# GpSimd multiplies one of eight state pairs with B in the scan of a four-layer image kernel

## The chip, the cores and the metric

The kernel runs on one core of one Trainium2 chip. The metric is the device time of one execution in microseconds. A core has five engines with queues of their own: TensorE (PE in the profile; PEld are its weight loads), VectorE (DVE), ScalarE (ACT), GpSimd (POOL) and SyncE (SP, which here issues the DMAs). Each engine works through its own queue in the order in which the program was written; semaphores order the work between engines.

## The reference

The input is 32 images of 128 channels and 56 x 56 pixels in fp32. Four layers follow one another, each as `x = x + layer(groupnorm(x))`: a dynamic convolution, a spline activation, a linear attention with a convolution, and a Mamba layer. The change lies in the fourth. Its core, for L = 3136 pixels taken as time, 256 inner channels d and 16 states n, is

```
delta = softplus(dt @ dt_proj_w.T + dt_proj_b)         # (L, 256)
dA    = exp(delta[..., None] * A)                      # (L, 256, 16)
dBu   = delta[..., None] * B_ssm[:, :, None, :] * xc[..., None]
h_t   = dA_t * h_{t-1} + dBu_t                         # the scan
y_t   = sum over n of h_t[d, n] * C_t[n]
```

The later `y + xc * D`, the gate `silu(z)` and the output projection follow on y.

## The kernel before

**Tiling.** An image is cut into 7 chunks of 448 pixels (CH, 8 rows of 56). Within a chunk the 256 channels x 16 states are worked off in 16 steps (STEPS): 8 pairs of states (NPAIR), and for each pair two blocks of 128 channels (DI). One step holds a tile h of 128 partitions x 2 x 448: partition halves of 64 are the two states of the pair, the middle index the two halves of the block's channels. 32 images x 7 chunks x 16 steps are 3584 steps.

**One step** (class Scan, lines 1041 to 1136). With `p, db = divmod(n, 2)`:

- `b_rows` (line 1069): once for each pair, a matmul with the selection matrix spreads the two B rows of the pair over the partitions, into the PSUM tile pb. Its pool ps_bc has one buffer (line 381).
- `c_rows` (line 1060): the same for C, into an mm tile (pool ps_mm, three buffers), which ScalarE copies to an SBUF tile cb (three buffers).
- `decay` (line 1076): ScalarE computes exp(delta * A) twice, 128x448 each, into two PSUM tiles da. Pool ps_da has two buffers, so a step takes both.
- `state` (line 1084): VectorE makes the product h = du * B over 128x896 (pb broadcast over the middle index; du is delta * xc), and then two scans over 448 in place, each with its da tile and the last value of the chunk before. h has three buffers.
- `products` (line 1100): ScalarE keeps the last column of h; GpSimd multiplies h with cb into hc (two buffers).
- `add` (line 1108): TensorE sums hc over the states into y, and at the end of the chunk VectorE applies the gate and TensorE the output projection.

Before the scan, `ssm_inputs` (line 1002) prepares a chunk: matmuls, silu, delta and du (GpSimd adds and multiplies 128x896 each) and, by DMA, the rearranged copies of delta and du that the steps read. `layer_norm` (line 964) prepares xn for the chunk after.

**Order of the work.** The loop over images (line 1284) takes six images a pass, and `images` (line 1196) writes the whole pass as a list of works: for each step the scan's own calls (lines 1254 to 1261), pieces of the next chunk's inputs, pieces of the next image's spline and attention layers, and pieces of the first layer of the image after that. Each work has a step and a lead (`plan.at(g, FIRST)`; FIRST is 8 steps, SECOND 4). The class Plan prices each work by engine and size (line 163), works out due times backward from the steps (line 232: a work is due its own cost ahead of whatever needs it), and then goes through a list schedule (`attempt`, line 245) with one queue for each engine and the buffers of each pool. Of the works that could start first on an engine the one with the earliest due time goes first; no work may be more than 12 steps ahead of the oldest one left. The result is a fixed order for each engine, which is issued at line 338; that is why nearly every row of the profile has line 338, and why rows are told apart by their tiles. Times at run time do not change the order.

Of the kernel before, what the change touches and what calls it, by code (L numbers as in the profile page):

```python
# [12 lines left out]
F32 = mybir.dt.float32  # L13
# [5 lines left out]
P = 128  # L19
# [3 lines left out]
CH = ROWS * W  # L23
# [31 lines left out]
DI = 2  # L55
# [4 lines left out]
B_ROW, C_ROW = 0, 64  # L60
# [6 lines left out]
NB = DI * P // Q  # L67
NPAIR = NST // 2
STEPS = NPAIR * DI
AHEAD = 2  # L70
LAG = 3
FIRST, SECOND = 8, 4
# [290 lines left out]
def tile_conv_stack(ctx: ExitStack, tc: tile.TileContext, out: bass.AP, x: bass.AP, w: dict):  # L363
    nc = tc.nc
# [4 lines left out]
    def pool(name, bufs, **kw):  # L369
        return Rotation(plan, ctx.enter_context(tc.tile_pool(name=name, bufs=bufs, **kw)), name, bufs)  # L370
# [5 lines left out]
    wide = pool("wide", 1)  # L376
    ssm = pool("ssm", 2)
    cbp = pool("cbp", 3)
    dramp = ctx.enter_context(tc.tile_pool(name="dramp", bufs=1, space=bass.MemoryType.DRAM))
    ps_mm = pool("ps_mm", 3, space=bass.MemoryType.PSUM)  # L380
    ps_bc = pool("ps_bc", 1, space=bass.MemoryType.PSUM)
# [179 lines left out]
    du = const.tile([P, DI, CH], F32, name="du")  # L561
# [18 lines left out]
    nc = plan  # L580

    def psum(cols=CH, rows=P):
        t = ps_mm.tile([P, 512], F32, tag="mm", name="mm")
        return t[:rows, :cols]


    class Stats:


        def __init__(self, xt, st=None):  # L590
            self.xt, self.done = xt, 0
            self.st = small.tile([P, NCH, 6], F32, tag="st", name="st") if st is None else st
# [399 lines left out]
    def gate(xn):  # L992

        for db in range(DI):
            ps = psum()
            nc.tensor.matmul(
                ps, wzT[:, db * P : (db + 1) * P], xn[:, DCONV - 1 :], start=True, stop=True
            )
            silu(sz[:, db, :], ps)
            yield 0.8  # L1000
# [40 lines left out]
    class Scan:  # L1041
# [3 lines left out]
        def __init__(self, xt, dst, last, k):  # L1045
            self.xt, self.dst, self.last, self.j, self.k = xt, dst, last, k % NCH, k
            self.dbl, self.xc = dbls[k % 2], xcs[k % 2]
            self.cbs, self.pbs, self.das, self.hcs, self.pys = {}, {}, {}, {}, {}

        def half(self, n):  # L1050

# [17 lines left out]
        def b_rows(self, n):  # L1069

            p, db = divmod(n, DI)
            if db == 0:
                self.pbs[p] = ps_bc.tile([P, 512], F32, tag="bc", name="pb")[:, :CH]
                self.both(self.pbs[p], B_ROW, p)

        def decay(self, n):
# [3 lines left out]
            for i in range(2):  # L1080
                b = 2 * db + i
                nc.scalar.activation(self.das[n][i], delta[:, i, :], AF.Exp, scale=amat[:, b, p : p + 1])

        def state(self, n):
            _, du = self.half(n)
            da = self.das.pop(n)
            h = ssm.tile([P, 2, CH], F32, tag="h", name="h", bufs=3)
            nc.vector.tensor_mul(h[:], du[:], self.pbs[n // DI].unsqueeze(1).to_broadcast([P, 2, CH]))
            for i in range(2):
                nc.vector.tensor_tensor_scan(  # L1090
                    h[:, i, :],
                    da[i],
                    h[:, i, :],
                    0.0 if self.j == 0 else self.last[:, n, i : i + 1],
                    ALU.mult,
                    ALU.add,
                )
            self.h = h

        def products(self, n):  # L1100
            h = self.h
            if self.j < NCH - 1:
                nc.scalar.copy(self.last[:, n, :], h[:, :, CH - 1])
            hc = ssm.tile([P, 2, CH], F32, tag="hc", name="hc", bufs=2)
            nc.gpsimd.tensor_mul(hc[:], h[:], self.cbs[n // DI][:].unsqueeze(1).to_broadcast([P, 2, CH]))
            self.hcs[n] = hc

        def add(self, n):
# [15 lines left out]
            if p == NPAIR - 1:  # L1124
                nc.vector.tensor_mul(sz[:, db, :], sz[:, db, :], self.pys[db])
            if n == STEPS - 1:
                cols = slice(self.j * CH, (self.j + 1) * CH)
# [5 lines left out]
        def store(self, n):  # L1133
            if n == STEPS - 1:
                cols = slice(self.j * CH, (self.j + 1) * CH)
                nc.sync.dma_start(self.dst[:, cols], self.xt[:, cols])


    def first_layer(src, b):

        xt = xts[b % 3]
        for j in range(NCH):
            nc.sync.dma_start(xt[:, j * CH : (j + 1) * CH], src[:, j * CH : (j + 1) * CH])
        yield from dynamic_conv(xt, sts[b % 2])

    def until_scan(b):

        xt = xts[b % 3]
        st = yield from spline(xt, sts[b % 2])
        st = yield from linear_attention(xt, st)  # L1150
        norm = carried[b % 2]
        norm_weights(st, *norm)
        yield 5.0
        layer_norm(xt, xns[b * NCH % 3], 0, norm)
        yield 5.0

    def first_inputs(b):
        return ssm_inputs(xts[b % 3], b * NCH, carried[b % 2])
# [37 lines left out]
    def images(first, count, ahead):  # L1196

        def image(v, b):  # L1200
            return v[:, ds(first + b, 1), :].squeeze(1)

        scans = {}

        def new_last():
            return small.tile([P, STEPS, 2], F32, tag="last", name="last")

        def at(g, what):

            if 0 <= g < count * NCH * STEPS:  # L1210
                getattr(scans[g // STEPS], what)(g % STEPS)

        plan.start(FIRST)

        for b in range(count):
            xt = xts[b % 3]
            steps = (NCH - 1) * STEPS + READY
            more = b + 1 < count or ahead
            rest = Pieces(until_scan(b + 1) if more else None, totals[1], REST)
            layer0 = Pieces(first_layer(image(xv, b + 2), b + 2) if b + 2 < count or ahead else None, totals[0], steps)  # L1220
            for j in range(NCH):
                k = b * NCH + j
                if k == 0:
                    last = new_last()
                    scans[0] = Scan(xt, image(ov, 0), last, 0)
                    for n in range(AHEAD):
                        at(n, "c_rows")
                    for n in range(2):
                        at(n, "b_rows")
                    at(0, "decay")  # L1230
                following = None
                if j + 1 < NCH:
                    following = ssm_inputs(xt, k + 1, carried[b % 2])
                elif more:
                    following = first_inputs(b + 1)
                following = Pieces(following, PREP, READY)
                gates = Pieces(gate(xns[k % 3]), 1.6, DI)
                for n in range(STEPS):
                    g = k * STEPS + n
                    plan.at(g)  # L1240
                    if n == 0 and j == NCH - 1:
                        rest.finish()
                    if n == READY:

                        following.finish()
                        gates.finish()
                        if j == NCH - 1:
                            layer0.finish()
                        if k + 1 < count * NCH:
                            nb, nj = divmod(k + 1, NCH)  # L1250
                            if nj == 0:
                                last = new_last()
                            scans[k + 1] = Scan(xts[nb % 3], image(ov, nb), last, k + 1)
                    plan.at(g, FIRST)
                    at(g + 2, "b_rows")
                    at(g, "state")
                    at(g + 1, "decay")
                    at(g, "products")
                    at(g + AHEAD, "c_rows")
                    at(g - LAG + 1, "add")  # L1260
                    at(g - LAG, "store")
                    plan.at(g, SECOND)
                    following.step(n)
                    if n >= READY - DI:
                        gates.step(n - READY + DI)
                    plan.at(g)
                    rest.step(j * STEPS + n)
                    if j * STEPS + n > LAG:
                        layer0.step(j * STEPS + n)
        end = count * NCH * STEPS  # L1270
        for g in range(end - LAG + 1, end):
            at(g, "add")
        at(end - 1, "store")
        plan.issue()
# [9 lines left out]
    with tc.For_i(0, B - 2, unroll) as i:  # L1284
        images(i, unroll, True)
    images(B - 2, 2, False)


# [100 lines left out]
```

## Time and profile before

| | |
|---|---|
| runs | 16321.42, 16330.96, 16344.79 us; median 16330.96 us |
| profiled execution | 16316.11 us, span from first to last instruction 16314.3 us |
| mean granted TensorE clock | 0.893 |
| steps | 3584, so 4.55 us of span each; a chunk takes some 72.8 us |
| matmul y<-hc,sums | 14336, 3997.9 us busy |
| decays da<-delta,alog on ScalarE | 7168, mean 633 ns, 4481.8 us busy |
| matmul pb<-dbl,sel | 1792, mean 512 ns |
| delta<-delta,du and du<-delta,xc on GpSimd | 224 each, mean 2093 and 2089 ns |
| DMA | 1589.93 MB, mean 97 GB/s |

How to read the profile: a group line gives line, engine, operation, the tiles out<-in, the shapes and the count; after the first bar the busy time in all and the mean of one in ns; after the second the engine's idle time just before such instructions and what ended most of it. A line of waits gives who waited for whom, the total in us, how often, and the longest. "hc<-h,cb" is the product with C, "h<-du,pb" the product with B, "h<-da,last,h" a scan.

### The profile page before, as it was taken

To read this page: it belongs to the slowest core of one execution; us is meant where nothing else is said; L and a number is where in the kernel's file an instruction comes from. 1 tells how busy PE (TensorE), PEld (TensorE's weight loads), DVE (VectorE), ACT (ScalarE), POOL (GpSimd) and SP (SyncE) were. 2 spreads that over 40 slices of the span, in tenths; PEclk is the share of its full clock that TensorE was granted. 3 is DMA by queue.
4 is the path that set the end of the run, shared out by engine and by line. 5 is a ranking of instruction groups with operands and counts; after the bars stand their busy time and mean duration, and the time that the engine had idled before them with its cause. 6 is when DMAs were issued, how large, how long until landed. Compare 5 with 4: busy or idle time off the path is not lost. (4 is left out here: it accounts for less than half of the span.)

```text
span 16314.3 us, 212520 instructions
## 1 busy us (share of the span) xinstructions
PE 14202.3 (87%) x66400; PEld 4559.9 (28%) x66400; DVE 14306.2 (88%) x17314; ACT 11713.4 (72%) x21127; POOL 10785.0 (66%) x6406
## 2 busy tenths in 40 slices
PE   6888898888898888988888888888888898888887
PEld 2222222222222222222222222222222222222222
DVE  2898988989889898899988888888898898888889
ACT  3777777777677776777776777767777677776675
POOL 2676666666666666667666666666676666766666
PEclk7888998889998898998989988899988899888888
DMA  6344444344443444434444434444344444344421
GB/s 143 93 101 98 98 112 96 89 99 101 106 104 88 100 97 101 109 94 94 101 99 107 102 86 98 99 105 107 91 98 97 100 108 106 85 97 99 101 56 34
DMA packets 986159, 1589.93 MB, mean 97 GB/s; under 512 B 175622, under 2 KB 611209, under 8 KB 984331
## 3 DMA queue, kind: packets, MB, share of 16 engines
q1 hardware_dynamic: 985002, 1576.06, 41.0%
q8 instruction: 538, 8.81, 0.2%
q14 instruction: 619, 5.06, 0.1%
HBM read 785.62 MB, written 173.18 MB: 59 GB/s over the span
## 5 line engine op out<-in xcount | busy, mean ns | idle before, releaser
L338 POOL TENSOR_TENSOR hc<-h,cb 128x896 f32<-128x896 f32 x3584 | 7476.1, 2092 | 4173.5 <-DVE h L338 2178.7
L338 DVE TENSOR_TENSOR_SCAN h<-da,last,h 128x448 f32<-128x448 f32 x6144 | 6772.7, 1135 | 498.2 <-ACT da L338 451.3
L338 ACT ACTIVATE da<-delta,alog 128x448 f32<-128x448 f32 x7168 | 4481.8, 633 | 2635.3 <-DVE h L338 2369.4
L338 PE MATMUL y<-hc,sums 128*64 128x448 f32 x14336 | 3997.9, 638 | 625.6 <-POOL hc L338 617.8
L338 DVE TENSOR_TENSOR h<-du,pb 128x896 f32<-128x896 f32 x3584 | 3788.6, 1072 | 247.5 <-POOL hc L338 118.2
L338 PE MATMUL mm<-stack,dsT 96*32 96x448 f32 (+1 forms) x16128 | 1890.8, 575 | 59.4 <-DMA stack<-padded 16.8
L338 ACT ACTIVATE hats<-stack,bia,scl 128x448 f32<-128x448 f32 x2688 | 1887.6, 754 | 33.9 <-DVE bia L338 31.7
L338 PE MATMUL mm<-xn,winT 128*128 128x448 f32 x3584 | 1703.8, 590 | 39.8 <-ACT cb L338 13.5
L338 PEld LDWEIGHTS y<-hc,sums 128*64 128x64 f32 x14336 | 807.6, 147 | 2412.9 <-POOL hc L338 1436.9
L338 PE MATMUL mm<-hats,wspl 128*32 128x448 f32 x12544 | 1386.1, 563 | 33.3 <-ACT hats L338 30.4
L338 PE MATMUL pb<-dbl,sel 64*128 64x448 f32 x1792 | 918.3, 512 | 421.2 <-DVE h L338 364.3
L338 ACT ACTIVATE hats<-hats,one 128x1344 f32<-128x1344 f32 x896 | 1261.5, 1408 | 0.1
L338 ACT COPY cb<-mm 128x448 f32<-128x448 f32 x1792 | 940.3, 527 | 379.4 <-POOL hc L338 184.0
L338 PE MATMUL mm<-dbl,sel 64*128 64x448 f32 x1792 | 892.3, 502 | 363.5 <-DVE sz L338 63.7
L338 ACT ACTIVATE t<-mm 128x448 f32<-128x448 f32 x1568 | 829.2, 534 | 484.6 <-PE mm L338 480.3
L338 POOL TENSOR_TENSOR xt<-xt,g 128x448 f32<-128x448 f32 x672 | 767.5, 1142 | 524.1 <-DVE g L338 491.1
L338 DVE TENSOR_TENSOR_SCAN h<-da,h 128x448 f32<-128x448 f32 x1024 | 1054.1, 1070 | 28.3 <-ACT da L338 26.3
L338 PEld LDWEIGHTS mm<-xn,winT 128*128 128x128 f32 x3584 | 631.8, 197 | 986.0 <-issue 805.1
L338 DVE SCALAR_TENSOR_TENSOR g<-t,mm 128x448 f32<-128x448 f32 x672 | 407.7, 607 | 443.7 <-ACT t L338 392.8
L338 PEld LDWEIGHTS mm<-stack,dsT 96*32 96x32 f32 (+1 forms) x16128 | 445.2, 112 | 1156.3 <-issue 899.9
L338 PEld LDWEIGHTS mm<-dbl,sel 64*128 64x128 f32 x1792 | 351.2, 198 | 1453.5 <-issue 420.0
L338 PEld LDWEIGHTS pb<-dbl,sel 64*128 64x128 f32 x1792 | 358.6, 200 | 1419.1 <-issue 791.8
(187 smaller groups left out, 16166.2 us busy)
## 6 DMA issues: line engine op xcount, KB each, us to landing
stack<-padded SPq DMA_DIRECT2D x2688, 264.0 KB
stack<-xt SPq DMA_DIRECT2D x3584, 56.0 KB
delta<-delta SPq DMA_DIRECT2D x1792, 112.0 KB
du<-du SPq DMA_DIRECT2D x1792, 112.0 KB
padded<-yc SPq DMA_DIRECT2D x224, 264.0 KB
padded<-yc SPq DMA_DIRECT2D x256, 231.0 KB
xt<-x_dram SPq DMA_DIRECT2D x224, 224.0 KB
out_dram<-xt SPq DMA_DIRECT2D x224, 224.0 KB
```

The costliest lines, as they stand in the source:

```text
L338: call()
```

## The change

A constant names the pairs that are treated in another way: pair 4 alone, which is steps 8 and 9 of each chunk. For it, the B rows go into an mm tile in place of pb, and ScalarE copies them to an SBUF tile bb (a new pool of one buffer). The product with B becomes a call of its own, `inputs`, taken out of `state`: for pair 4 it runs on GpSimd and reads bb, for the other pairs it runs on VectorE and reads pb as before. For all pairs the call now stands one step earlier in the list, between the scans of step g and the decays of step g + 1. The tile h is kept by step in a dictionary in place of one variable.

```diff
+ASIDE = (4,)
...
+    bbp = pool("bbp", len(ASIDE))
...
         def b_rows(self, n):
             p, db = divmod(n, DI)
-            if db == 0:
+            if db == 0 and p in ASIDE:
+                ps = psum()
+                self.both(ps, B_ROW, p)
+                self.bbs[p] = bbp.tile([P, CH], F32, tag="bb", name="bb")
+                nc.scalar.copy(self.bbs[p][:], ps)
+            elif db == 0:
                 self.pbs[p] = ps_bc.tile([P, 512], F32, tag="bc", name="pb")[:, :CH]
                 self.both(self.pbs[p], B_ROW, p)
...
+        def inputs(self, n):
+
+            _, du = self.half(n)
+            h = self.hs[n] = ssm.tile([P, 2, CH], F32, tag="h", name="h", bufs=3)
+            if n // DI in ASIDE:
+                nc.gpsimd.tensor_mul(h[:], du[:], self.bbs[n // DI][:].unsqueeze(1).to_broadcast([P, 2, CH]))
+            else:
+                nc.vector.tensor_mul(h[:], du[:], self.pbs[n // DI].unsqueeze(1).to_broadcast([P, 2, CH]))
+
         def state(self, n):
-            _, du = self.half(n)
             da = self.das.pop(n)
-            h = ssm.tile([P, 2, CH], F32, tag="h", name="h", bufs=3)
-            nc.vector.tensor_mul(h[:], du[:], self.pbs[n // DI].unsqueeze(1).to_broadcast([P, 2, CH]))
+            h = self.hs[n]
...
-            self.h = h
 
         def products(self, n):
-            h = self.h
+            h = self.hs.pop(n)
...
                     for n in range(2):
                         at(n, "b_rows")
+                    at(0, "inputs")
                     at(0, "decay")
...
                     at(g + 2, "b_rows")
                     at(g, "state")
+                    at(g + 1, "inputs")
                     at(g + 1, "decay")
                     at(g, "products")
```

More of the change, by code (lines that the diff above doesn't have):

```diff
@@ L1047, in __init__ @@
             self.dbl, self.xc = dbls[k % 2], xcs[k % 2]
-            self.cbs, self.pbs, self.das, self.hcs, self.pys = {}, {}, {}, {}, {}
+            self.cbs, self.bbs, self.pbs, self.das, self.hs, self.hcs, self.pys = {}, {}, {}, {}, {}, {}, {}
         def half(self, n):
```

## Prediction

> **What bounds the kernel now.** I read the page from the top: busy shares, then the chain of work that ended last, then the costliest groups.
>
> ```profile
> PE 14202.3 (87%) x66400; PEld 4559.9 (28%) x66400; DVE 14306.2 (88%) x17314; ACT 11713.4 (72%) x21127; POOL 10785.0 (66%) x6406
> ...
> DVE 9%; PE 6%; ACT 4%; issue 2%; POOL 2%; DMA 0%; SPq 0%; POOLq 0%; DVEq 0%; ACTq 0%
> ...
> L338 POOL TENSOR_TENSOR hc<-h,cb 128x896 f32<-128x896 f32 x3584 | 7476.1, 2092 | 4173.5 <-DVE h L338 2178.7
> L338 DVE TENSOR_TENSOR_SCAN h<-da,last,h 128x448 f32<-128x448 f32 x6144 | 6772.7, 1135 | 498.2 <-ACT da L338 451.3
> L338 DVE TENSOR_TENSOR h<-du,pb 128x896 f32<-128x896 f32 x3584 | 3788.6, 1072 | 247.5 <-POOL hc L338 118.2
> L338 ACT COPY cb<-mm 128x448 f32<-128x448 f32 x1792 | 940.3, 527 | 379.4 <-POOL hc L338 184.0
> ```
>
> VectorE and TensorE are both near 88% and GpSimd has a third of its time free. The chain goes back only over the last pass of the image loop and the two images after it, so its shares add up to some 24% of the span; of what it covers, VectorE holds 9 of 24 parts, TensorE 6, ScalarE 4, GpSimd 2. No single engine is the bound. Next come the waits of VectorE and TensorE:
>
> ```profile
> PE y L338 <- POOL hc L338: 617.8, 697, 6.3
> PE pb L338 <- DVE h L338: 364.3, 360, 15.8
> ...
> DVE h L338 <- ACT da L338: 478.9, 503, 3.0
> ...
> DVE h L338 <- POOL hc L338: 118.2, 93, 3.0
> ...
> DVE h L338 <- PE pb L338: 88.7, 115, 1.9
> ```
>
> The scans wait for the decays 503 times; the products with B wait rarely, for a free h buffer (GpSimd) or for pb (TensorE). Last, the table by stretches of one typical chunk (image 20, second chunk), cut at the starts of the products of steps 0, 6, 8, 10 and the next chunk's 0; each pair is busy us and instructions, for PE, PEld, DVE, ACT and POOL:
>
> ```profile
> 10494.22:10514.72 20.50, 19.89 (x106) 6.46 (x105) 20.50 (x29) 16.35 (x31) 14.23 (x10) 1.00 0.23 57
> 10514.72:10525.04 10.32, 6.24 (x18) 1.90 (x16) 10.32 (x19) 10.32 (x20) 6.86 (x4) 0.82 0.00 1
> 10525.04:10535.35 10.31, 9.65 (x23) 3.43 (x24) 10.19 (x14) 8.74 (x16) 6.39 (x4) 0.68 0.28 68
> 10535.35:10562.00 26.65, 20.41 (x94) 5.53 (x92) 21.68 (x25) 24.47 (x43) 21.02 (x14) 0.88 0.40 99
> ```
>
> Pair 4 is the third row (steps 8 and 9): VectorE is full there and GpSimd is idle for 3.9 of 10.3 us. I ordered all rows of the trace by step: over all chunks of the loop, steps 7 to 11 last 22.4 us, of which VectorE is idle 2.0 and GpSimd 9.4; in steps 12 to 14 GpSimd is idle only 1.2 of 14.8 us, because the next chunk's delta, du and xn fall there. So the chosen pair lies in a stretch where VectorE is short and GpSimd is not.
>
> **What the Trainium skill says.** "GPSIMD Engine Reference", section "Performance versus the Vector engine": a two-input elementwise instruction takes about 1.96 times as long on GpSimd. The trace agrees: 2092 ns against 1072 ns for the same 128x896 shape, 1.95. "PSUM — Partial Sum Buffer", section "PSUM: the matmul accumulator": GpSimd can't touch PSUM; hence the copy to SBUF. "Advanced Engine Details and Errata", section "Miscellaneous Facts": GpSimd shares an SBUF interface with VectorE and conflicts with VectorE instructions that have two SBUF inputs. Here the products and scans each have one operand in PSUM, and hc stays between 2061 and 2151 ns; but the small aggT<-dwT,attr,aggT on VectorE takes 0.33 us alone and 1.22 us beside an hc, so the conflict is visible on small rows. "Perfetto Trace Analysis", section "Per-instruction lifecycle": ScalarE, VectorE and GpSimd are strict FIFOs, so a late product holds back every hc behind it.
>
> **The change part by part**, against the profiled run (16316.1 us, span 16314.3; the median of the runs is 14.9 us higher).
>
> 1. VectorE loses one pair in eight: 3584 / 8 = 448 products. Start to start, a product followed at once by another instruction takes 0.998 us (median over the trace), so 447 us of VectorE work go. That all of it shows is the upper end. The nearer figure comes from the chain: in the last pass of the loop (2948 us) the chain spends 388 us in steps 8 and 9, 137 of them in h on VectorE. A product is 1.00 of 1.00 + 2 x 1.06 us of a step's h work, 0.32, so 44 us, 1.49% of the pass; times 16314 that is 243 us. With the order of work fixed the gain can't be more than that. The order isn't fixed (the planner writes it anew), and of the remaining 204 us of free VectorE time I let a quarter, 50 us, come to use. Taken: -293 us; ends -447 and 0.
>
> 2. GpSimd gains 448 x 2.092 = 937 us (busy 66% to 72%). Most lies in its idle time. Its share on the path: hc holds 3.4% of the chain in that pass and is busy 46% of the span, a ratio of 0.074, so 69 us. The conflicts with VectorE: its small rows with two SBUF inputs (vv 78, aggT 69, dm 36, ab 34, att 29 us: 246) grow with GpSimd's busy time, 937/10785 or 9%; half of the 21 us, 10. Taken: +79; ends 0 and the case of lateness below.
>
> 3. ScalarE gains 224 copies (32 images x 7 chunks), priced by the cb copy of the same shape: 224 x 0.527 = 118 us (72% to 72.5%). ScalarE holds some 15% of the chain and is busy 72%, ratio 0.21: 25 us. Behind the copy in ScalarE's queue stand decays, and behind those the scans. Taken +25; ends 0 and 118.
>
> 4. Between a step's scans and the next stood a product of 1 us, under which ScalarE made the next decays (633 ns each, and only as a scan frees one of the two PSUM buffers). In two steps of 16 this cover goes. Now 503 of 3584 steps wait, 0.95 us each; if in the 448 steps the share rises from 14% to about 30%, this is 448 x 0.16 x 0.95 = 68 us, of which other VectorE work fills half: +34. Ends 0 and 200 (half of them wait 0.95 us).
>
> 5. Buffers. The matmul for pair 4 goes from the single bc buffer to one of three mm buffers. Credit: an eighth of the pb waits, 11 us of VectorE and 45 of TensorE; debit: an mm buffer is held about 1 us once a chunk. I take 0; ends -30 and +30.
>
> 6. The products of all pairs are now issued a step earlier, ahead of that step's decays: their due time falls by some 2 us of plan (from 2.4 us ahead of the step to 4.5), still after the scans of the step before, so scans keep their precedence. Three h buffers as before. No DMA and no SP work moves; hc, delta and du stay on GpSimd, but can queue behind a product. Taken 0; ends -50 and +50, as any new order shifts things.
>
> Sum: -293 + 79 + 25 + 34 = -155 us on 16316, so 16161; plus the 14.9 of the median: **16176 us**, 0.95% below 16331.
>
> **Rivals.** (B) VectorE is the true bound and the planner fills every hole: -447, and the additions at half (+69): 16331 - 378 = **15953**. For it: VectorE idles only 2 us in steps 7 to 11. Against: TensorE is busy 87% as well, and of h's busy time on VectorE (71% of the span) only some 42% lies on the chain (29.6% of the pass). (C) What comes free is filled by waits for decays and by TensorE (item 4 at its end, +200 in place of +34): 16331 - 155 + 166 = **16342**, no change. For it: 8% of the chain is issue, 20% TensorE's mm, which the change doesn't touch. (D) The slower one: the product of step 9 is late on GpSimd. It needs an h buffer that the hc of step 6 gives back; now VectorE starts that product 2.86 us after this release (median), in 17% of chunks at once. On GpSimd it takes 2.09 instead of 1.00 us. Free at the release, it is in time in the median chunk; behind one hc it is 4.18 - 3.86 = 0.3 us late, behind two 2.4 us. If two is the rule, 224 x 2.4 = 538 us of scan waits; VectorE fills half with other work, 269: 16331 - 155 + 269 = **16445**. It decides from 155 / (224 x 0.5) = 1.4 us of lateness per chunk. For it: strict FIFO, 45% of chunks with less than 2.3 us of slack. Against: 9.4 us of GpSimd idle time in steps 7 to 11 against 4.2 needed. That the change doesn't do what it says I can exclude: pair 4 is plainly taken by the new branch.
>
> **How the numbers follow.** Forecast 0.48, B 0.18, C 0.12, D 0.22. About 0.2% (33 us) is what a measurement of this kernel can tell from no change; forecast and B are faster by more, C is within it, D is slower: 0.66, 0.12, 0.22. The range reaches from below B, 15900, to D, 16445: outside are D's upper half (0.11) and B's tail (0.04). The cases faster than before have their own range, 15900 to 16290.
>
> **What would show it.** Products h<-du,pb x3136, a GpSimd h<-du,bb x448 near 2092 ns, copies bb<-mm x224 near 527; VectorE busy near 13,860, GpSimd near 11,720, ScalarE near 11,830. Item 4: the wait of h for da grows from 478.9 by under 100. Item 2 and D: a new wait of VectorE's scans for GpSimd's h; under 100 us speaks for the forecast, over 300 for D. If TensorE's idle time falls by as much as the span, B holds. I am wrong in the main step if VectorE's busy time falls by 447 and its idle time grows by as much.

## The result, and the profile after

The change makes the kernel slower: 16700.19 us median against 16327.31 us, a ratio of 1.0223 with a 95% interval of 1.0208 to 1.0237. The forecast was 16176 us and the range ended at 16445. In the page of the kernel after, busy shares, chain and the groups that were shown of before:

```profile
PE 14197.5 (85%) x66400; PEld 4568.4 (27%) x66400; DVE 14067.0 (84%) x16866; ACT 11829.0 (71%) x21351; POOL 11693.9 (70%) x6854
...
PE 8%; DVE 7%; ACT 5%; POOL 2%; issue 2%; SPq 0%; DMA 0%; DVEq 0%; POOLq 0%; ACTq 0%
...
L339 POOL TENSOR_TENSOR hc<-h,cb 128x896 f32<-128x896 f32 x3584 | 7472.1, 2091 | 3443.0 <-DVE h L339 1734.6
L339 DVE TENSOR_TENSOR_SCAN h<-da,last,h 128x448 f32<-128x448 f32 x6144 | 6770.7, 1137 | 779.3 <-ACT da L339 427.3
...
L339 DVE TENSOR_TENSOR h<-du,pb 128x896 f32<-128x896 f32 x3136 | 3320.7, 1072 | 302.5 <-POOL hc L339 179.3
...
L339 ACT COPY cb<-mm 128x448 f32<-128x448 f32 x1792 | 940.8, 527 | 286.1 <-PE mm L339 185.3
...
L339 POOL TENSOR_TENSOR h<-du,bb 128x896 f32<-128x896 f32 x448 | 936.2, 2091 | 152.2 <-issue 74.5
```

The work has moved as the change says: 448 products at 2091 ns on GpSimd, 3136 left on VectorE. The large instructions take as long as before. Yet VectorE, relieved of 468 us of products, is idle for 2637 us in place of 2008. The waits of the kernel after say where the idle time shows:

```profile
PE y L339 <- POOL hc L339: 869.9, 714, 11.3
...
DVE h L339 <- ACT da L339: 505.8, 494, 7.5
...
DVE h L339 <- POOL h L339: 304.7, 180, 4.5
...
DVE h L339 <- POOL hc L339: 179.3, 158, 3.9
```

Scans now wait 305 us for GpSimd's products, and TensorE's matmuls of y wait 252 us longer for hc. Both can cost time, but the loss is not only where these waits are. By step (from first scan to first scan, mean over all chunks inside the run) a chunk grew from 71.4 to 73.0 us, and steps 2, 3, 11 and 14, far from pair 4, grew by 0.35 to 0.57 us each, while steps 7 to 10, around pair 4, grew by less than 0.5 us together. The planner had written all queues anew: apart from the products with B, of 2550 VectorE instructions in one pass of the loop only some 1040 stand at the same place in the queue as before. So two theories were open. **L:** the slower product and the added work on GpSimd hold up scans and hc. **O and M:** the new order costs, either as any new draw of the order would (O) or because the products of all pairs are due a step earlier (M).

### The profile page after: what moved, and what is told of

Read it like the earlier page. It is cut to its first block, busy times and chain, and to the rows that moved or that the text cites. A ratio compares the mean times of both kernels' runs of the same rounds, so it can differ in the third digit from the quotient of the medians.

```text
span 16703.7 us, 211721 instructions
## 1 busy us (share of the span) xinstructions
PE 14197.5 (85%) x66400; PEld 4568.4 (27%) x66400; DVE 14067.0 (84%) x16866; ACT 11829.0 (71%) x21351; POOL 11693.9 (70%) x6854
## 5 line engine op out<-in xcount | busy, mean ns | idle before, releaser
L339 POOL TENSOR_TENSOR hc<-h,cb 128x896 f32<-128x896 f32 x3584 | 7472.1, 2091 | 3443.0 <-DVE h L339 1734.6
L339 DVE TENSOR_TENSOR h<-du,pb 128x896 f32<-128x896 f32 x3136 | 3320.7, 1072 | 302.5 <-POOL hc L339 179.3
L339 PE MATMUL mm<-stack,dsT 96*32 96x448 f32 (+1 forms) x16128 | 1932.3, 587 | 57.2 <-DMA stack<-onesd 20.0
L339 PE MATMUL mm<-hats,wspl 128*32 128x448 f32 x12544 | 1440.9, 581 | 43.8 <-ACT hats L339 30.8
L339 PE MATMUL mm<-dbl,sel 64*128 64x448 f32 x2016 | 950.1, 499 | 321.0 <-DVE sz L339 87.3
L339 PE MATMUL pb<-dbl,sel 64*128 64x448 f32 x1568 | 805.2, 514 | 322.0 <-DVE h L339 280.9
L339 POOL TENSOR_TENSOR h<-du,bb 128x896 f32<-128x896 f32 x448 | 936.2, 2091 | 152.2 <-issue 74.5
L339 PE MATMUL mm<-xn,wzT 128*128 128x448 f32 x896 | 555.7, 709 | 293.5 <-DVE g L339 151.0
```

Source lines behind the costliest of these rows:

```text
L339: call()
```

## Experiments

**1. The parts one by one.** First the move alone: no pair is put aside.

```diff
-ASIDE = (4,)
+ASIDE = ()
-    bbp = pool("bbp", len(ASIDE))
+    bbp = pool("bbp", 1)
```

> The kernel after with no pair put aside: all products on VectorE again, but each called one step earlier, and the whole order written anew by the planner. Theory M (the earlier call of the products is what costs): 16600 to 16750, as slow as after. Theory O (what costs is the order that the planner happens to write, whatever makes it write anew): any value from 16150 to 16700, not tied to the GpSimd product. Theory L (the product is late on GpSimd and holds scans and hc up): 16330 within 50.

Measured: 16800.77 us, ratio 1.0289 (1.0272 to 1.0306). All products are on VectorE, and it is slower than after and above all three ranges, so a loss needs no product on GpSimd. With the due time left at step g + 1 and only the place in the list changed, the planner writes the order of before in the loop, instruction for instruction (this variant was not run): what redraws the order is the due time. Next the other part alone: each product called in its own step again.

```diff
                     at(g + 2, "b_rows")
+                    at(g, "inputs")
                     at(g, "state")
-                    at(g + 1, "inputs")
```

> The kernel after, but each product called in its own step as in before; pair 4 stays on GpSimd. Theory M: back to 16330 or below. Theory L: 16700 within 70, since GpSimd does the same products from the same queue. Theory O: off from after by over 80 to either side, since the planner writes another order.

Measured: 16590.22 us, 1.0158 (1.0135 to 1.0181). Each part alone is slower than before, by 465 and 255 us, and both together are slower by 373: the parts don't add up. Neither M's nor L's mark for this run was met; O's was, since the run is 110 us off after.

**2. The order held still.** A planner's order can be kept while an instruction changes its engine: the plan is made with the product on VectorE, and only the call behind the planned work is exchanged. Every queue then has the sequence of before, except that 448 products stand on GpSimd, at the place in time that the plan gave them, and that ScalarE has 224 more copies of B to SBUF, each behind its matmul.

```diff
-                self.both(self.pbs[p], B_ROW, p)
+                with plan.together():
+                    self.both(self.pbs[p], B_ROW, p)
+                    if p == 4:
+                        self.bb = bbp.tile([P, CH], F32, tag="bb", name="bb")
+                        plan.group.calls.append(partial(tc.nc.scalar.copy, self.bb[:], self.pbs[p]))
...
-            nc.vector.tensor_mul(h[:], du[:], self.pbs[n // DI].unsqueeze(1).to_broadcast([P, 2, CH]))
+            wide = [P, 2, CH]
+            call = None
+            if n // DI == 4:
+                call = partial(tc.nc.gpsimd.tensor_mul, h[:], du[:], self.bb[:].unsqueeze(1).to_broadcast(wide))
+            plan.add("vector", "tensor_mul", (h[:], du[:], self.pbs[n // DI].unsqueeze(1).to_broadcast(wide)), {}, call)
```

> The order of before kept instruction for instruction on every queue, with only the 448 products of pair 4 taken from VectorE's queue and put on GpSimd's at the place which the plan of before gives them, and the copy of B to SBUF behind its matmul. Theory O: no loss, 16100 to 16350, since VectorE is relieved and nothing else moves. Theory L: slower than before by over 200, since a product of 2.09 us stands before the scans and ahead of hc in an order that was made for one of 1.07 us on VectorE.

Measured: 16916.58 us, 1.0365 (1.0348 to 1.0383). Theory O's no loss is refuted for this order. The traces show that the order was kept: apart from products with B and copies of B, all rows of VectorE, ScalarE and GpSimd stand in the sequence of before. Since the order is the same, the same chunk can be laid beside the table in the prediction (image 20, second chunk; cut at the products of steps 0, 6, 8, 10 and the next 0; busy us of PE, PEld, DVE, ACT, POOL):

```profile
10863.46:10885.81 22.35, 21.08 (x100) 6.40 (x101) 20.77 (x28) 15.75 (x30) 14.32 (x10) 0.85 0.21 52
10885.81:10896.13 10.32, 6.60 (x19) 1.98 (x17) 10.32 (x19) 9.24 (x18) 6.25 (x3) 0.82 0.00 0
10896.13:10907.49 11.36, 9.46 (x22) 3.23 (x22) 8.67 (x11) 10.49 (x20) 11.31 (x6) 0.65 0.24 56
10907.49:10934.14 26.65, 20.66 (x96) 5.91 (x94) 21.61 (x24) 24.55 (x43) 20.55 (x14) 0.88 0.41 101
```

In pair 4 (third row) GpSimd went from 6.39 busy of 10.31 us to 11.31 of 11.36: it has become full there, and VectorE went from 10.19 busy to 8.67. GpSimd's rows of this stretch in order of time show what is in its queue (start, us, operation, idle time before and who ended it):

```profile
10893.55 2.08 POOL L338 TENSOR_TENSOR hc<-h,cb 128x896 f32<-128x896 f32 x1 [1.44 <-DVE h L338]
10896.17 2.08 POOL L338 TENSOR_TENSOR h<-du,bb 128x896 f32<-128x896 f32 x1 [0.54 <-ACT bb L338]
10898.24 1.87 POOL L338 TENSOR_SCALAR ind<-xt,top,cpad 128x448 f32<-128x448 f32 x1
10900.08 2.09 POOL L338 TENSOR_TENSOR h<-du,bb 128x896 f32<-128x896 f32 x1
10902.12 6.17 POOL L338 TENSOR_TENSOR hc<-h,cb 128x896 f32<-128x896 f32 x3
```

The second product stands behind the spline's ind (1.87 us), and three hc, 6.17 us without a pause, have piled up behind it: this is the strict FIFO of the prediction at work. Over all chunks the product of step 8 ends 3.70 us after the scans of the step before (2.50 in before) and that of step 9 2.09 us (0.33); in 68% and 63% of cases a scan starts within 0.2 us of it, so the cover is used up. By step, 2.5 of the 2.65 us that a chunk grows lie in steps 7 to 10 (+0.71, +1.09, +0.45, +0.25), and no other step changes by more than 0.14. The waits of this kernel put both ways of loss side by side, VectorE's for the product and TensorE's for hc (617.8 in before):

```profile
PE y L338 <- POOL hc L338: 909.8, 794, 5.1
...
DVE h L338 <- POOL h L338: 486.1, 255, 4.0
```

This is theory L, at its place.

**3. The relief alone.** In the same order the products of pair 4 are left out and the scans read du. There is no copy of B here.

```diff
             nc.vector.tensor_mul(h[:], du[:], self.pbs[n // DI].unsqueeze(1).to_broadcast([P, 2, CH]))
+            left_out = n // DI == 4
+            if left_out:
+                plan.works[-1].calls = []
...
-                    h[:, i, :],
+                    (du if left_out else h)[:, i, :],
```

> The order of before kept, and the products of pair 4 left out altogether (the two scans of each such step read du in place of du times B, so this part of the computation is missing). It prices the relief of VectorE alone. The chain of before gave at most 243 us for a fixed order: 16090 or above, if that reading holds; if VectorE is the true bound there, 447: near 15885. Under 50 us would mean that VectorE's product was not on the path in pair 4.

Measured: 16228.19 us, 0.9942 (0.9925 to 0.9958): taking 447 us of VectorE's time away gives 107 us. That is within the 243 us read from the chain, and less than half of it. VectorE's scans now wait longer for the decays (478.9 us in before):

```profile
DVE h L338 <- ACT da L338: 592.1, 543, 3.0
```

GpSimd's products and the copies that feed them cost 16916.58 - 16228.19 = 688 us in this order.

**4. Load or lateness?** The products stay on VectorE, and GpSimd makes hc twice in steps 8 and 9: the same added work, behind the scans.

```diff
             nc.gpsimd.tensor_mul(hc[:], h[:], self.cbs[n // DI][:].unsqueeze(1).to_broadcast([P, 2, CH]))
+            if n // DI == 4:
+                plan.works[-1].calls *= 2
```

> The order of before, all products on VectorE, but GpSimd makes hc twice in steps 8 and 9: the same 448 x 2.09 us of added work on GpSimd as in the change, behind the scans and not ahead of them. If added work on GpSimd costs wherever it stands (it pushes hc, the matmuls of y and the free h buffers): 16700 or more. If the cost of the change is that a scan waits for its product: 16330 to 16480.

Measured: 16853.00 us, 1.0322 (1.0305 to 1.0339). My theory that it is the wait of the scan for its product falls as the whole story: 937 us of added work on GpSimd cost 520 us with no scan waiting for a GpSimd product. The waits of this kernel show the way round, and its row of products with B after them:

```profile
PE y L338 <- POOL hc L338: 1031.9, 761, 5.3
...
ACT cb L338 <- POOL hc L338: 263.4, 190, 5.4
DVE h L338 <- POOL hc L338: 228.5, 217, 3.3
DVE h L338 <- PE pb L338: 218.5, 159, 3.3
```

```profile
L338 DVE TENSOR_TENSOR h<-du,pb 128x896 f32<-128x896 f32 x3584 | 3800.3, 1074 | 527.7 <-POOL hc L338 228.5 <-PE pb L338 218.5 <-PE mm L338 33.7
```

TensorE waits 1031.9 us for hc (617.8 in before). Its matmuls start in the written order (66386 of 66400 rows stand at the same place in both traces), so what stands behind the matmuls of y waits too, the matmul of the next pb among them: VectorE's wait for pb rises from 88.7 to 218.5 us, that for a free h from 118.2 to 228.5. Its idle time before products with B grows by 280 us (247.5 to 527.7), the largest part of the 475 us by which its idle time grows in all. So an hc that GpSimd makes late costs in two ways, through TensorE's queue and through the h buffers, even where GpSimd has idle time on average.

**5. Other pairs in the old order.** The same exchange for pairs 0 and 6 (`p == 0`, `p == 6`).

> As the run with pair 4 in the old order, but pair 0 (steps 0 and 1) goes to GpSimd. In before the two products of pair 0 end 1.07 and 1.82 us ahead of their scans (pair 4: 1.04 and 1.15), and hc starts 0.45 us after its scans (pair 4: 1.5), so GpSimd has no backlog there. If lateness of the product is what costs and its price follows from cover and backlog: less than half of the 581 us of pair 4, 16350 to 16620. If GpSimd's work as such costs, wherever it is: near 16900.

> As before, with pair 6 (steps 12 and 13), where in before the products end 3.80 and 2.93 us ahead of their scans, but GpSimd is busy 91 to 95%. If the time by which the product leads its scans decides (cover): 16300 to 16550. If GpSimd's backlog decides: the worst of the three pairs, over 16950.

Measured: 16933.08 us, 1.0376 (1.0359 to 1.0394), and 17102.12 us, 1.0482 (1.0465 to 1.0500). Both times most of the loss lies at the pair's own steps (pair 0: +0.96, +1.01, +0.21 us in steps 15, 0, 1; pair 6: +1.77 and +0.60 in steps 12 and 13). My expectation for pair 0, less than half of pair 4's loss, is wrong, and so is cover as the rule: it would have favoured pair 6, which is the worst, where GpSimd was 91 to 95% busy. What came true is "GpSimd's work as such, near 16900" for pair 0 and "backlog" for pair 6. So GpSimd's added work cost 520 us or more in each of the four places tried in the old order, and most where GpSimd was fullest; a rule that gives its size was not found.

**6. How much is an order worth?** Four kernels have exactly the instructions of before, in other orders: a scan's price per element at 2.09e-3 for 2.085e-3, STEP at 4.45 for 4.5, VectorE's HOP at 0.25 for 0.17, WINDOW at 11 for 12.

> The kernel before, with one price of the planner nudged by a quarter of a per cent (a scan's price per element 2.09e-3 in place of 2.085e-3); the instructions are the same ones, in another order. If the order that the planner happens to write is worth per cents by itself (theory O): off from 16330 by over 100 to either side. If a small change of order costs nothing and it is the earlier due time of the products that costs 465 us (theory M): 16330 within 50.

> The kernel before, with the planner's length of a step nudged by one per cent (4.45 in place of 4.5), so that all due times move a little; same instructions, another order. Theory O: off from 16330 by over 100 to either side. Theory M: 16330 within 50.

> The kernel before with the planner's time from VectorE to another engine at 0.25 in place of 0.17 us: the same instructions, but an order that differs from that of before about as much as that of the move alone does. If any order that far from before costs per cents (before is a lucky draw, theory O): 16500 to 16900. If the early due time of the products is a cause of its own (theory M): 16250 to 16450.

> The kernel before with the planner's window at 11 steps in place of 12: again the same instructions in an order of its own. Theory O: 16500 to 16900. Theory M: 16250 to 16450.

Measured: 16373.40 (1.0035, interval 1.0022 to 1.0047), 16372.99 (1.0035, 1.0023 to 1.0048), 16607.91 (1.0171, 1.0154 to 1.0188) and 16630.71 us (1.0183, 1.0166 to 1.0200). Before is the best of five draws. The two small nudges stayed within some 50 us of it, as theory M had it; the two larger ones came out at 16600 and above, as theory O had it. The same price nudge on the move alone and on after:

> The move alone (all products on VectorE, called one step earlier), with the scan's price nudged by a quarter of a per cent so that the planner writes yet another order. Theory M (the earlier due time as such): 16800 within 100 again. Theory O (one bad draw): anywhere from 16330 to 16800, likely nearer to 16500.

> The kernel after with the same nudge. If its 2.2% is systematic: 16700 within 100. If it is a draw: off by more.

Measured: 16659.47 (1.0201, 1.0184 to 1.0218) and 16689.68 us (1.0223, 1.0206 to 1.0240). The move alone came out 141 us better for a quarter of a per cent in one price, which speaks for a draw; after stayed within 11 us, as its 2.2% being systematic would have it. A last order has only GpSimd's products due a step earlier:

```diff
+                    plan.at(g + ((g + 1) % STEPS // DI not in ASIDE), FIRST)
                     at(g + 1, "inputs")
+                    plan.at(g, FIRST)
```

> The kernel after, but only the GpSimd products are due a step earlier; those of VectorE are due in their own step as in before. If the earlier due time helps a slow product and harms the fast ones: below 16590, 16400 to 16560. If only the draw of the order matters: anywhere between 16500 and 16750.

Measured: 16874.61 us, 1.0337 (1.0320 to 1.0354), over 300 above what I expected of the better of both parts, and above the range for a mere draw too. Reasoning from one due time to the result does not work here.

**7. The order of after held still.** As in 2 and 3, but in the order of after. First the products of pair 4 are left out (the scans of these steps read du, by the same edit as in 3):

```diff
                 nc.gpsimd.tensor_mul(h[:], du[:], self.bbs[n // DI][:].unsqueeze(1).to_broadcast([P, 2, CH]))
+                plan.works[-1].calls = []
```

> The order of after kept on every queue, with the 448 products of pair 4 left out on both engines (the scans of steps 8 and 9 read du in place of du times B, so this part of the computation is missing; the copy to SBUF stays). If the 373 us of after come from GpSimd's work (theory L): it falls by 400 or more, to 16100 to 16300. If they come from the new order as such (theory O or M): 16550 or above.

Then they are made on VectorE, where bb is the broadcast copy of B that GpSimd read:

```diff
+                plan.works[-1].calls = [partial(tc.nc.vector.tensor_mul, h[:], du[:], bb)]
```

> The order of after kept, with the products of pair 4 made on VectorE at the place where the plan of after has GpSimd make them (operands du and bb, both in SBUF). Theory L: faster than after, 16350 to 16600, since 937 us of GpSimd's work go. Theory O or M: 16700 or more, since VectorE gets the 447 us back in an order that left no room for them.

Measured: 16527.30 (1.0119, 1.0102 to 1.0135) and 16875.81 us (1.0331, 1.0314 to 1.0349). The first lies just under the mark for the order as such (16550) and far above that for GpSimd's work (16300); the second is within O's and M's (16700 or more). In this order GpSimd's products cost 173 us over none, and VectorE's 349. That GpSimd is the better place in this order by 176 us doesn't follow: with two SBUF operands a VectorE product took 1392 ns in the mean in place of 1072, 143 us in all, and held up GpSimd's hc by as much (see the end). But without any product this order takes 16527, where that of before takes 16228; the copies of B, which stay in the one and are missing in the other, are in this difference.

**8. Like against like.** After, under the two larger nudges.

> The kernel after with the nudge of the run with the hop at 0.25, to be set beside that run (16608) and not beside before. If the change has a cost of its own in an order drawn at random of the size it has against before: 16980. If before is a lucky draw and the change itself is worth about nothing: 16600 within 150. If the relief of VectorE shows once both orders are drawn alike: 16300 to 16450.

> The kernel after with the window at 11, to be set beside the run of before with that window (16631). Own cost: 17000. About nothing: 16630 within 150. Relief: 16350 to 16480.

Measured: 16770.40 (1.0256, 1.0239 to 1.0273) and 16999.93 us (1.0395, 1.0377 to 1.0413). Four pairs of draws, each with and without the change under the same planner constants:

| constants | without | with | difference |
|---|---|---|---|
| as given | 16327 | 16700 | +373 |
| scan price | 16373 | 16690 | +316 |
| hop | 16608 | 16770 | +162 |
| window | 16631 | 17000 | +369 |

The change is slower in all four, by 305 us in the mean (before itself ran at 16331 us beside the runs without and at 16348 beside those with the change in the last two rows, so 17 us of each may be the group's). One came out at the mark for a cost of the change's own (17000, window), the other between the marks (16770, hop). Before's good draw is not the reason by itself: under all four sets of constants the change costs.

## Why the prediction was wrong

The path from before to after can be walked with the order held still on each side, in us:

| kernel | order | products of pair 4 | time |
|---|---|---|---|
| before (medians of all groups) | old | VectorE | 16323 to 16348 |
| experiment 3 | old | none | 16228 |
| experiment 2 | old | GpSimd | 16917 |
| experiment 7 | new | none | 16527 |
| after | new | GpSimd | 16700 |

From before (16335, beside experiments 2 and 3) there are two walks. Over the old order: -107 for the relief, +688 for GpSimd's products with their copies, -216 for the new order. Over the new order: -107, then +299 for the new order with the copies, then +173 for GpSimd's products. Both end at +365. The price of each part depends on the other, and the prediction had priced GpSimd's work at 69 us and the order at nothing.

**Item 1, the relief.** Predicted 293 us; measured 107 in the old order (16335 - 16228, its own runs of before). The term read from the chain, 243, was called the most that can be gained, and then all of it was taken, with 50 us added for reordering. Less than half came: when the product goes, VectorE waits elsewhere, most of all for the decays (+113 us in experiment 3).

**Item 2, GpSimd's added work.** This is the first step that failed: "hc holds 3.4% of the chain in that pass and is busy 46% of the span, a ratio of 0.074, so 69 us". In the old order it costs 688 us (experiment 2 less 3, copies included), and 520 with no scan behind it (experiment 4); in the order made for it 173. The ratio took the added work to lie on the chain as seldom as hc does; but the added work made its own path, over the scans and over hc. GpSimd's idle 3.9 us of 10.3 in pair 4 and 9.4 in steps 7 to 11 were an average; in the chunk shown the products of 4.2 us filled the stretch and three hc piled up behind. The conflict on small VectorE rows, put at 10 us, was undersized as well: in the old order dm<-mv,mg alone went from 35.9 to 92.2 us.

**Item 6, the order.** Predicted 0 with ends of 50 us, without a run behind it. It is the other failed term: the new order, with the copies, costs 16527 - 16228 = 299 us where both have no products of pair 4, and orders of the same instructions span 16327 to 16801. The copies can't be told apart here: ScalarE is busy 117 us with them, priced at 25 in item 3. The due time moved by "some 2 us of plan" kept scans ahead of products, as I argued; but the planner takes at each point the earliest work of each engine and never goes back, so that one exchange can change what follows (argued from its code; that the order did change is measured). With GpSimd's products in it the new order is the better one, by 216 us (16916.6 to 16700.2).

**Items 3, 4, 5.** The copy is as priced (ScalarE +116 us busy, 11829.0). The wait for da grew by 27 us, under the 100 allowed; but in the old order, with the products gone, it grew by 113, so the small figure seems owed to the new order. Item 5 was not tested by itself; VectorE's wait for pb fell from 88.7 to 59.8 us.

**Rivals.** D named the right mechanism, strict FIFO on GpSimd and scans waiting for its h; its mark (over 300 us of such waits) is met at 304.7. But it looked only at VectorE's scans and left out the way over hc, TensorE's queue and pb, which costs 520 us by itself in experiment 4; how after's loss divides between the two ways isn't shown. D left the order out too; 16445 was 255 us short. VectorE's busy time fell by 239 us and not by 447, since other rows ran longer (dm<-mv,mg by 101 us), and its idle time rose by 629: in sense, though not to the number, the line "I am wrong in the main step if" came true.

**What stays open.** Which property makes the order of before good was not found. The copies of B were never run without the products. That orders as far from it cost 1.7 to 2.9% is shown; whether the earlier due time costs by itself can't be told: the move alone came out 465 us above before, and 286 us above its partner under the price nudge (16659 against 16373), which are only two draws.

## What to carry to other kernels

In a kernel whose queues are written by a planner, a change can be two changes, the work that moves and the order that is redrawn; keep the planned order and exchange the call to price the first, nudge a constant of the planner to price the second, and compare pairs of draws. An engine with a third of its time free isn't free where it stands in a loop with in-order queues: price added work by the stretch in which it falls and by who waits in order behind it, not by its share of the chain, which here was 2.3 times what a removal gained (243 against 107 us) and far below what an addition cost (69 against 173 to 688 us). Even so its size had to be measured.

## What the runs showed of the hardware

TensorE's busy time isn't fixed by its work: the same 66400 matmuls were busy 14202.3 us at a mean granted clock of 0.893 in before, and 14483.0 us at 0.872 with the move alone. In after they were busy 14197.5 us at 0.885, no longer than in before, so TensorE's own speed doesn't explain after's loss. Whether the lower clock of the move alone is a cause or a result of its longer time was not tested.

```profile
PE 14483.0 (86%) x66400; PEld 4672.7 (28%) x66400; DVE 14390.7 (86%) x17314; ACT 11739.6 (70%) x21127; POOL 10791.7 (64%) x6406
```

The Trainium skill's "Advanced Engine Details and Errata", section "Miscellaneous Facts", on the SBUF interface that GpSimd and VectorE share, and on VectorE instructions with two SBUF inputs, holds for large instructions as well. In the second kernel of experiment 7, where VectorE's product has both operands in SBUF, its rows (min/median/max in ns, then those of GpSimd's hc in the same run) are

```profile
L339 DVE TENSOR_TENSOR h<-du,bb x448: 1054/1073/3008, 465.0 to 16805.3; 128x896 f32<-128x896 f32 x150
```

```profile
L339 POOL TENSOR_TENSOR hc<-h,cb x3584: 2063/2092/2971, 446.3 to 16862.8; 128x896 f32<-128x896 f32 x200
```

against maxima of 1090 and 2151 ns in before, where VectorE's second operand is in PSUM:

```profile
L338 DVE TENSOR_TENSOR h<-du,pb x3584: 1023/1076/1090, 436.0 to 16300.1; 128x896 f32<-128x896 f32 x200
```

```profile
L338 POOL TENSOR_TENSOR hc<-h,cb x3584: 2061/2091/2151, 441.9 to 16304.0; 128x896 f32<-128x896 f32 x200
```

The engine that comes second seems to wait for the other's whole instruction: 142 of the 448 products took over 1.2 us, and ended 0.95 us (median) after the GpSimd instruction that was running when they started, about a whole product of their own; 211 hc took over 2.2 us, and ended 1.94 us after VectorE's product. This also hits small instructions. The 128 instructions dm<-mv,mg, of one column each, took 36 us in all in before and 137 in after:

```profile
L338 DVE TENSOR_TENSOR dm<-mv,mg 128x1 f32<-128x1 f32 x128 | 35.9, 281 | 0.7
```

```profile
L339 DVE TENSOR_TENSOR dm<-mv,mg 128x1 f32<-128x1 f32 x128 | 137.4, 1073 | 0.5
```

In after 52 of them met an hc (82 us) and 30 a product with B on GpSimd (49 us). The new order alone, without these products (experiment 7), made it 76 us.
